# Sorting the last half lot of a mixture-of-experts layer through HBM instead of by matrix products

## The chip, the cores and the metric

The kernel runs on one core of one Trainium2 chip. The metric is the device time of one execution in microseconds (us), as the median over runs. TensorE (PE in the profile) multiplies matrices, VectorE (DVE) and ScalarE (ACT) do elementwise work, GpSimd (POOL) does a few elementwise operations and issues the indirect DMAs, and SyncE (SP) issues all plain DMAs of the main part. PEld is TensorE's weight load. A TensorE product of float32 leaves two records in the trace, a transpose one.

## The reference, cut to what matters

The input `x` is 8 sequences of 256 rows of 128 numbers, 2,048 rows in all. Four residual layers follow one another, each on a layer norm of its input: an attention with 8 heads (called a), a mixture of experts, a second attention with 16 heads (called b), and the same mixture of experts again with the same weights.

```python
x = x + attn_a(_layernorm(x, axis=-1), Mq, Mk, Mv)
x = x + ffn(_layernorm(x, axis=-1), w_gate, b_gate, W1, b1, W2, b2)
x = x + attn_b(_layernorm(x, axis=-1), wq, w_down, wk_up, wv_up, wo)
x = x + ffn(_layernorm(x, axis=-1), w_gate, b_gate, W1, b1, W2, b2)

def ffn(x, w_gate, b_gate, W1, b1, W2, b2):      # x_flat: rows of 128
    logits = x_flat @ w_gate + b_gate            # 8 experts
    probs = softmax(logits)
    route_p, route_idx = max(probs), argmax(probs)
    h = relu(einsum('nd,edm->enm', x_flat, W1) + b1[:, None, :])   # 512 wide
    y = einsum('enm,emd->end', h, W2) + b2[:, None, :]
    return y[route_idx, arange(n)] * route_p[:, None]
```

Only one expert's result is kept for a row, so the kernel computes each row for its own expert alone. For that the rows have to be put in order by expert, and the results have to be put back.

## The kernel before, in words

**Tiling.** The rows form four groups of 512 (two sequences, four tiles of 128 rows). Attention a runs over the groups, then attention b. A lot is what one call of `ffn_pieces` takes. The first mixture of experts takes each group as a lot (tiles named `..._f`). The second (`..._e`) takes groups 0, 1 and 2 as lots of four tiles, and group 3 as two half lots of two tiles, one for each sequence, as each sequence leaves attention b by itself. I call these five lots e0, e1, e2, e30 and e31. e31 is the last; `last` is true for it alone.

**A lot.** Layer norm (`layernorm_T`: `bn_stats`, a power on POOL that gives `rstd`, then `shift`, `hf` on ACT, transposes `pt`, a copy `hT`), gate products `pg`, a dozen small DVE operations that find each row's expert (`lg`, `mx`, `eq`, `sc`, `m2`, `sums`), two products `before` that count earlier rows of the same expert, and from them a place `ps_` for each row. Each expert has room for `CAP` rows (128 in a lot of four tiles, 64 in a half lot). A row that finds no room raises `over`, from which `find_most` (product `pov`) and `load_most` make a flag; if it is set, a branch at the end (`tc.If`) computes everything again without sorting. In the runs here that branch isn't taken.

**Sorting through HBM** (every lot but e31). `in_memory` makes two HBM buffers and writes zeros into the first (`tx`), by SP. POOL issues one indirect DMA for each tile that writes the rows of `h` to their places in `tx` (a put); SP loads `tx` back as `rows`, in order; `turned` transposes `rows` to `rTs` (products `prt`). Then come eight experts: `hidden` (products `H`, results `h1` on DVE or ACT) and `project` (products `py`, results `ys` on DVE). SP writes `ys` to the second HBM buffer (`ox`) in two halves, and POOL fetches each tile's results with an indirect DMA (`yg`, a gather). DVE adds them to the input (`x_e`), and SP stores the rows.

**Sorting by products** (e31 only, `sorted_here`). DVE compares a row of numbers (`place`) with each row's place and gives a matrix `has` of zeros and ones, 128 x 512 for each of the two tiles. Two products of `h` with `has` give the sorted, transposed rows at once. `has` is transposed (`pht`) and copied to `comes`; at the end, eight products `pn` of `comes` with `ys` put the results back. No HBM buffer, put, `rows` or gather is used. As `place` counts through experts with 64 places each, `ps_` is computed with `direct` (a step of 64 places between experts) instead of `region` (256).

**The order.** All instructions are issued in an order that is written out when the kernel is built. `Plan` holds an estimated clock for every engine and for DMA. Attention b is the main thread (`flow_b`); everything else, lots included, is a `Side`: a generator that yields the time at which its next piece is due. `fill` and `reach` step the ripe side of the best rank into the main thread. Where the plan's TensorE clock shows a gap, `busy` puts products of `ident` into a PSUM tile `spare`, whose result nobody reads. Each engine then runs its own list strictly in that order. So a change of a lot's steps changes the plan's clock, and with it the order and the spare products of everything after. `ranks[0] = rank` and `computed` hold a lot's experts back until the earlier lot's are done; `computed[0] < turn - 1` holds the load of `rows` back until the lot two before is done.

In attention b, `largest` and `exps` make score products (`S_b`, `ST_b`), DVE takes maxima (`top`), ACT exponentials (`bex`), `values` makes `acc_b`; `divide` turns `acc_b` into a new residual: ACT copies it to `both_b`, eight DMAs move the sums into `den_b` (in the last entry the products `pd_b` do this instead), DVE takes the reciprocal and forms `yT_b`, PE makes `py_b` and DVE `x_b`.

Of the kernel before, what the change touches and what calls it, by code (L numbers as in the profile page):

```python
# [24 lines left out]
def kernel(  # L25
# [29 lines left out]
    B, T, D = x.shape  # L55
    E, _, FF = W1.shape
# [149 lines left out]
    const = Pool("const", 1)  # L206
    xp = Pool("xp", 7)
    ln = Pool("ln", 2)
# [9 lines left out]
    class Ordered:  # L218
# [27 lines left out]
    PE, DVE, ACT, POOL = (  # L246
        Ordered(engine, name)
        for engine, name in (
            (nc.tensor, "pe"), (nc.vector, "dve"), (nc.scalar, "act"), (nc.gpsimd, "pool")
        )  # L250
    )

    def load(out, src):

        plan.dma(out, src, "sp")
        return tc.keep_in_program_order(nc.sync.dma_start(out, src))

    def misc(name):
        return pm.tile([P, 512], F32, tag="m", name=name)
# [60 lines left out]
    ident = const.tile([P, P], F32, tag="ident", name="ident")  # L320
# [3 lines left out]
    mark = const.tile([1, 1], F32, tag="mark", name="mark")  # L324
# [19 lines left out]
    ROWS = {4: 128, 2: 64}  # L344
# [2 lines left out]

    region = {n: const.tile([P, E], F32, tag=f"region{n}", name=f"region{n}") for n in ROWS}
    closer = {n: const.tile([P, E], F32, tag=f"closer{n}", name=f"closer{n}") for n in ROWS}
    direct = const.tile([P, E], F32, tag="direct", name="direct")  # L350
    place = const.tile([P, E * ROWS[2]], F32, tag="place", name="place")
    b1T = const.tile([P, E * NM], F32, tag="b1T", name="b1T")
    b2T = const.tile([P, E], F32, tag="b2T", name="b2T")
    nb1T = const.tile([P, E * NM], F32, tag="nb1T", name="nb1T")

    def setup_experts():
        steps = [(direct, ROWS[2])]
        for n, rows in ROWS.items():
            steps += [(region[n], n * P), (closer[n], rows - n * P)]
        for t, step in steps:  # L360
            DVE.tensor_scalar(t, first, -float(step), float(step * E), ALU.mult, ALU.add)
        count = mid.tile([P, E * ROWS[2]], I32, tag="both", name="count", bufs=1)
        POOL.iota(count, [[1, E * ROWS[2]]], base=0, channel_multiplier=0)
        POOL.tensor_copy(place, count)

        pb = misc("pb")
        PE.transpose(pb[:, 0 : E * NM], b_rows[: E * NM, 0, :], ident[: E * NM, : E * NM])
        PE.transpose(pb[:, 64 : 64 + E], b_rows[:E, 1, :], ident[:E, :E])
        ACT.copy(b1T, pb[:, 0 : E * NM])
        ACT.copy(b2T, pb[:, 64 : 64 + E])  # L370
        DVE.tensor_scalar(nb1T, b1T, -1.0, None, ALU.mult)
# [162 lines left out]
    def hop():  # L534

        return plan.end + plan.HOP
# [37 lines left out]
    def soon():  # L574
        return plan.at["pe"] + 1.0
# [328 lines left out]
    begun_ffn, computed, ended_ffn = [0], [0], [0]  # L904
# [24 lines left out]
    def in_memory(n, NL):  # L929
        to_expert = hbm.tile([E, NL * P, D], F32, tag=f"tx_{n}", name=f"tx_{n}")  # L930
        of_expert = hbm.tile([E * ROWS[NL], D], F32, tag=f"ox_{n}", name=f"ox_{n}")
        for nothing, to in by_expert(zeros.unsqueeze(1).to_broadcast([P, E, D]), to_expert):
            load(to, nothing)
        return to_expert, of_expert

    def ffn_pieces(turn, n, tokens, ended, vector_norm, ranks, rank, last):
        NL = sum(tiles for _, tiles in tokens)
        TL, CAP = NL * P, ROWS[NL]
        PT = 2 * CAP // P
        sorted_here = last  # L940
        if not sorted_here:
            to_expert, of_expert = in_memory(n, NL)
        while any(name not in x_of for name, _ in tokens) or turn - ended_ffn[0] >= LOTS:
            yield soon()
        h = ln.tile([P, ML, D], F32, tag="hf", name=f"hf_{n}", bufs=2)
# [5 lines left out]
        def row(name, dt=F32):  # L951
            t = sm.tile([P, ML], dt, tag=f"r{name}", name=f"{name}_{n}", bufs=LOTS)
            return t[:, 0:NL]
# [4 lines left out]
        def over_tiles(t, tiles=NL):  # L958
            return t.unsqueeze(1).to_broadcast([P, tiles, E])

        lg, d, sc, ex, rk = (small(s) for s in ("lg", "d", "sc", "gex", "rk"))
# [3 lines left out]
        eq = eqs[:, 0:NL, :]  # L965
# [17 lines left out]
        mx, m2, den, pr, ps_ = (row(s) for s in ("mx", "m2", "gden", "pr", "pos"))  # L983
# [14 lines left out]
        for lhsT, of, start in ((earlier, eqs, True), (ones, sums, False)):  # L998
            PE.matmul(
                before, lhsT=lhsT, rhs=of.rearrange("p n e -> p (n e)"), start=start,  # L1000
                stop=not start,
# [1 line left out]
        counts = before[:, NL * E : (NL + 1) * E]  # L1003
        DVE.tensor_tensor(
            rk, before[:, : NL * E].rearrange("p (n e) -> p n e", e=E),
            over_tiles(direct if sorted_here else region[NL]), ALU.add,
        )
        DVE.tensor_tensor(rk, rk, eq, ALU.mult)
        DVE.tensor_reduce(ps_, rk, AX.X, ALU.add)
        DVE.scalar_tensor_tensor(over, counts, -float(CAP), over, ALU.add, ALU.max)  # L1010
        if not sorted_here:
            pos = row("posi", I32)
            DVE.tensor_scalar(pos, ps_, float(E * TL - 1), None, ALU.min)
        if last:
            find_most()
        yield hop()
        if not sorted_here:
            puts = []
            for i in range(NL):

                POOL.memset(mark, 0.0)
                put = POOL.indirect_dma_start(
                    out=to_expert.rearrange("e c d -> (e c) d"),
                    out_offset=bass.IndirectOffsetOnAxis(ap=pos[:, i : i + 1], axis=0),
                    in_=h[:, i, :],
                    in_offset=None,
                )
                for other in puts:
                    tc.declare_no_dep(put.ins, other.ins, reason="rows of their own")
                puts.append(put)  # L1030
            yield hop()
            while computed[0] < turn - 1:
                yield soon()
            rows = ln.tile([P, E, D], F32, tag="rows", name=f"rows_{n}", bufs=3)
            for to, some in by_expert(rows, to_expert):
                load(to, some)
            loaded = hop()
            yield


        POOL.tensor_tensor(d, lg, wide(mx), ALU.subtract)
        if not sorted_here:
            POOL.tensor_tensor(rk, eq, over_tiles(closer[NL]), ALU.mult)
        yield hop()
        ACT.activation(ex, d, AF.Exp)
        if not sorted_here:
            DVE.tensor_reduce(m2, rk, AX.X, ALU.add)
            DVE.tensor_tensor(m2, m2, ps_, ALU.add)
            pos2 = row("posi2", I32)
            DVE.tensor_scalar(pos2, m2, float(E * CAP - 1), None, ALU.min)  # L1050
        yield hop()
        DVE.tensor_reduce(den, ex, AX.X, ALU.add)
        DVE.reciprocal(pr, den)
        yield None if sorted_here else loaded

        ranks[0] = rank
        while computed[0] < turn or not ready["bias"].over or not ready["turned"]:
            yield soon()
        rTs = {}
        if sorted_here:  # L1060

            has = ln.tile([P, NL, E * CAP], F32, tag="rows", name=f"has_{n}", bufs=3)
            for i in range(NL):
                DVE.tensor_scalar(has[:, i, :], place, ps_[:, i : i + 1], None, ALU.is_equal)
            yield hop()
            pt = misc(f"prt_{n}")
            for i in range(NL):
                PE.matmul(
                    pt, lhsT=h[:, i, :], rhs=has[:, i, :], start=(i == 0), stop=(i == NL - 1)
                )  # L1070
            rTs[0] = ln.tile([P, 512], F32, tag="rT", name=f"rT_{n}")
            ACT.copy(rTs[0], pt)
            yield
            comes = ln.tile([P, NL, E * CAP], F32, tag="rows", name=f"comes_{n}", bufs=3)
            for i in range(NL):
                pt = misc(f"pht_{n}_{i}")
                for k in range(E // 2):
                    PE.transpose(pt[:, ts(k, P)], has[:, i, ts(k, P)], ident)
                (DVE.tensor_copy, ACT.copy)[i % 2](comes[:, i, :], pt)
                yield  # L1080
        ys = ln.tile([P, E, D], F32, tag="rows", name=f"ys_{n}", bufs=3)
        stored = [0.0]

        def turned(t0):
            pt = misc(f"prt_{n}_{t0}")
            for i in range(4):
                PE.transpose(pt[:, ts(i, P)], rows[:, t0 + i, :], ident)
            copy = DVE.tensor_copy if vector_norm else ACT.copy
            rTs[t0 // 4] = ln.tile([P, 512], F32, tag="rT", name=f"rT_{n}_{t0}")
            copy(rTs[t0 // 4], pt)  # L1090

        def hidden(e):
            h1 = big.tile([P, NM, P], F32, tag="h1r", name=f"h1_{n}_{e}", bufs=4)
# [69 lines left out]
        if sorted_here:  # L1163
# [4 lines left out]
            for i in range(NL):  # L1168
                pn = misc(f"pn_{n}_{i}")[:, 0:D]
                for k in range(E // 2):  # L1170
                    PE.matmul(
                        pn, lhsT=comes[:, i, ts(k, P)], rhs=ys[:, k, :],
                        start=(k == 0), stop=(k == E // 2 - 1),
# [432 lines left out]
```

## Time and profile before

| what | value |
|---|---|
| time, median of 3 runs (lowest to highest) | 489.77 us (487.17 to 495.07) |
| time of the profiled execution | 486.11 us |
| its span, first to last instruction | 484.3 us |
| mean granted clock of TensorE | 0.994 |
| TensorE busy in slices 36 to 40 of 40 (tenths) | 8, 8, 8, 9, 6 |
| HBM traffic | 13.57 MB read, 10.88 MB written, 50 GB/s over the span |
| puts `tx_e`: issued on POOL, first to last start | 14, 305.8 to 439.1 us |
| gathers `yg_e`: on POOL, median us from issue to landing | 14, 2.5 us |
| layer norm's power on POOL for a half lot (`rstd_e`, 128x2) | 0.73 and 0.70 us |

A timeline line in the sections below gives start, duration, engine, line of the code, operation, output <- inputs, shapes and count; the bracket gives the engine's idle time before it and what ended that. All operations on PE, DVE, ACT and POOL bear line 227 (the helper `call` that records them) and all of SP's line 256, so groups are told apart by tile names. "SPq" is a DMA's issue on SP; the landing isn't in its duration.

### The profile page before, as it was taken

Reading aid. Unit: us, or ns where it says so; the run is one execution under the profiler, and the core shown is the slowest. Engines: PE = TensorE matmul, PEld = TensorE weight load, DVE = VectorE, ACT = ScalarE, POOL = GpSimd, SP = SyncE. Lnnn points to the kernel's source line nnn. Section 1 sums busy time; section 2 is a strip of 40 time slices with the busy share of each in tenths; the row PEclk is TensorE's granted clock in tenths of the full one; section 3 lists DMA queues with packets and bytes.
Section 4 is the critical chain, followed back from the end, with each engine's and each line's share of the span. In section 5 each row is a group of like instructions: output and inputs, shape, how many; then the busy total and the mean of one; then the engine's idle time right before and its main releaser. Section 6 shows DMA issues by size and latency. Waiting matters only on the chain.

```text
span 484.3 us, 13563 instructions
## 1 busy us (share of the span) xinstructions
PE 448.7 (93%) x5578; PEld 357.8 (74%) x5578; DVE 300.2 (62%) x816; ACT 223.2 (46%) x638; POOL 167.4 (35%) x249
## 2 busy tenths in 40 slices
PE   8899999999989899999999989989988999888996
PEld 7567775798567689787788667658776878577985
DVE  3555966953484937767756868667855867264231
ACT  2377454633364490456545446355634453242321
POOL 3032435542550565245430463413453002502310
PEclk9999999999999999999999999899999999999998
DMA  7980000103110002211131001010014101202210
GB/s 213 337 211 11 3 3 24 47 1 93 34 51 1 2 24 68 86 36 35 33 90 33 23 23 56 25 54 3 11 45 113 32 22 46 76 24 77 56 33 19
DMA packets 40550, 26.33 MB, mean 54 GB/s; under 512 B 3640, under 2 KB 37856, under 8 KB 40480
## 3 DMA queue, kind: packets, MB, share of 16 engines
q1 hardware_dynamic: 38560, 21.44, 15.2%
q0 software_dynamic: 1920, 3.94, 2.9%
q8 instruction: 46, 0.75, 0.6%
q14 instruction: 24, 0.20, 0.1%
HBM read 13.57 MB, written 10.88 MB: 50 GB/s over the span
## 4 chain that ended last, share of the span: by engine, by line
PE 68%; DVE 18%; ACT 8%; issue 4%; SPq 1%; POOL 0%; DMA 0%; another core or an unknown queue 0%; DVEq 0%; ACTq 0%; POOLq 0%
PE ST_b L227 8%; PE py_e L227 7%; PE H_e L227 6%; PE pq_a L227 6%; PE acc_b L227 5%; PE H_f L227 5%; PE S_a L227 4%; PE py_f L227 4%; PE spare L227 4%; PE S_b L227 3%; DVE nmax_a L227 3%; PE prot_b L227 3%; ACT ex_a L227 3%; DVE den_b L227 2%; DVE top L227 2%
## 5 line engine op out<-in xcount | busy, mean ns | idle before, releaser
L227 ACT ACTIVATE bex_b<-ST_b 128x768 f32<-128x768 f32 x64 | 51.9, 814 | 91.2 <-PE S_b L227 72.0
L227 DVE TENSOR_REDUCE top<-S_b 128x2 f32<-128x512 f32 (+1 forms) x128 | 65.1, 552 | 39.5 <-PE S_b L227 26.9
L227 ACT ACTIVATE ex_a<-S_a,nmax_a 128x256 f32<-128x256 f32 x128 | 58.9, 481 | 45.4 <-DVE nmax_a L227 37.7
L227 PE MATMUL ST_b<-qT_b,kT_b 32*128 32x128 f32 (+1 forms) x512 | 67.0, 352 | 4.2 <-issue 2.5
L227 PEld LDWEIGHTS ST_b<-qT_b,kT_b 32*128 32x128 f32 x512 | 49.5, 186 | 18.8 <-issue 9.7
L227 PE MATMUL S_b<-kT_b,qT_b 32*128 32x128 f32 (+1 forms) x512 | 59.8, 351 | 1.6 <-DVE top L227 1.5
L227 POOL TENSOR_TENSOR vh_a<-vs_a,rden_a 128x512 f32<-128x512 f32 x32 | 33.2, 1039 | 79.4 <-DVE rden_a L227 53.6
L227 PE MATMUL spare<-ident 128*128 128x128 f32 x364 | 51.2, 291 | 1.6 <-POOL ident masks.py:199 1.4
L227 PEld LDWEIGHTS spare<-ident 128*128 128x128 f32 x364 | 46.2, 202 | 5.0 <-issue 2.7
L227 PEld LDWEIGHTS S_b<-kT_b,qT_b 32*128 32x128 f32 x512 | 46.4, 186 | 4.5 <-issue 4.1
L227 DVE TENSOR_REDUCE nmax_a<-S_a 128x4 f32<-128x1024 f32 x32 | 38.7, 1211 | 13.3 <-PE S_a L227 13.2
L227 PE MATMUL H_e<-rT_e,W_sb 128*128 128x128 f32 (+1 forms) x320 | 40.7, 278 | 1.6 <-ACT rT_e L227 1.3
L227 PEld LDWEIGHTS H_e<-rT_e,W_sb 128*128 128x128 f32 x320 | 37.6, 192 | 3.8 <-ACT rT_e L227 1.8
L227 PE MATMUL S_a<-qT_a,kT_a 64*128 64x256 f32 x256 | 36.5, 402 | 2.5 <-ACT ex_a L227 1.6
L227 PE MATMUL py_e<-W_sb,h_e 128*128 128x128 f32 (+1 forms) x320 | 35.3, 278 | 0.9 <-DVE qT_b L227 0.9
L227 ACT ACTIVATE h_e<-H_e,b1T 128x128 f32<-128x128 f32 (+1 forms) x80 | 20.9, 350 | 32.3 <-PE H_e L227 32.3
L227 PE MATMUL H_f<-rT_f,W_sb 128*128 128x128 f32 x256 | 33.2, 280 | 2.0 <-DVE rt_b L227 1.1
L227 PEld LDWEIGHTS py_e<-W_sb,h_e 128*128 128x128 f32 (+1 forms) x320 | 32.4, 170 | 2.1 <-DVE qT_b L227 1.0
L227 PEld LDWEIGHTS H_f<-rT_f,W_sb 128*128 128x128 f32 x256 | 30.3, 192 | 4.6 <-issue 1.6
L227 PE MATMUL py_f<-W_sb,h_f 128*128 128x128 f32 x256 | 31.7, 278 | 0.4 <-issue 0.4
L227 PE MATMUL acc_b<-bex_b,vz 128*32 128x128 f32 (+1 forms) x512 | 29.9, 338 | 1.5 <-issue 1.4
L227 PEld LDWEIGHTS py_f<-W_sb,h_f 128*128 128x128 f32 x256 | 29.8, 192 | 1.6 <-issue 1.2
(220 smaller groups left out, 776.4 us busy)
## 6 DMA issues: line engine op xcount, KB each, us to landing
W_sb<-in_L_ffn_W_dram SPq DMA_DIRECT2D x16, 256.0 KB, 5.9
tx_f<-zeros SPq DMA_DIRECT2D x4, 512.0 KB, 6.9
rows_f<-tx_f SPq DMA_DIRECT2D x4, 512.0 KB
ox_f<-ys_f SPq DMA_DIRECT2D x8, 256.0 KB, 2.4
tx_e<-zeros SPq DMA_DIRECT2D x3, 512.0 KB
rows_e<-tx_e SPq DMA_DIRECT2D x3, 512.0 KB
ox_e<-ys_e SPq DMA_DIRECT2D x6, 256.0 KB, 2.5
x_in<-in_L_attn_a_x_dram SPq DMA_DIRECT2D x4, 256.0 KB, 3.7
```

Source lines behind the costliest of these rows:

```text
L227: return tc.keep_in_program_order(getattr(self.engine, op)(*args, **kw))
```

## The change

The last half lot gets its rows in order through HBM as the others do: `in_memory` is called for it, it makes puts, loads `rows` and transposes them with `turned(0)`. Its results still go by products: `has`, `comes` and `pn` stay. `has` now compares `place` with `m2` (the place in steps of 64, the sum of `ps_` and `closer`) instead of `ps_`; `direct` goes. `pos2`, the store to `ox` and the gathers stay left out for it. `turned` only moves upwards in the function.

```diff
-    direct = const.tile([P, E], F32, tag="direct", name="direct")
...
-        steps = [(direct, ROWS[2])]
+        steps = []
...
         sorted_here = last
-        if not sorted_here:
-            to_expert, of_expert = in_memory(n, NL)
+        to_expert, of_expert = in_memory(n, NL)
...
-            over_tiles(direct if sorted_here else region[NL]), ALU.add,
+            over_tiles(region[NL]), ALU.add,
...
-        if not sorted_here:
-            pos = row("posi", I32)
-            DVE.tensor_scalar(pos, ps_, float(E * TL - 1), None, ALU.min)
+        pos = row("posi", I32)
+        DVE.tensor_scalar(pos, ps_, float(E * TL - 1), None, ALU.min)
         if last:
             find_most()
         yield hop()
-        if not sorted_here:
-            puts = []
...
+        puts = []
+        for i in range(NL):
+
+            POOL.memset(mark, 0.0)
+            put = POOL.indirect_dma_start(
+                out=to_expert.rearrange("e c d -> (e c) d"),
+                out_offset=bass.IndirectOffsetOnAxis(ap=pos[:, i : i + 1], axis=0),
+                in_=h[:, i, :],
+                in_offset=None,
+            )
...
+        yield hop()
+        while computed[0] < turn - 1:
+            yield soon()
+        rows = ln.tile([P, E, D], F32, tag="rows", name=f"rows_{n}", bufs=3)
+        for to, some in by_expert(rows, to_expert):
+            load(to, some)
+        loaded = hop()
+        yield
...
-        if not sorted_here:
-            POOL.tensor_tensor(rk, eq, over_tiles(closer[NL]), ALU.mult)
+        POOL.tensor_tensor(rk, eq, over_tiles(closer[NL]), ALU.mult)
         yield hop()
         ACT.activation(ex, d, AF.Exp)
+        DVE.tensor_reduce(m2, rk, AX.X, ALU.add)
+        DVE.tensor_tensor(m2, m2, ps_, ALU.add)
         if not sorted_here:
-            DVE.tensor_reduce(m2, rk, AX.X, ALU.add)
-            DVE.tensor_tensor(m2, m2, ps_, ALU.add)
             pos2 = row("posi2", I32)
...
-        yield None if sorted_here else loaded
+        yield loaded
...
         if sorted_here:
+            turned(0)
+            yield
 
             has = ln.tile([P, NL, E * CAP], F32, tag="rows", name=f"has_{n}", bufs=3)
             for i in range(NL):
-                DVE.tensor_scalar(has[:, i, :], place, ps_[:, i : i + 1], None, ALU.is_equal)
+                DVE.tensor_scalar(has[:, i, :], place, m2[:, i : i + 1], None, ALU.is_equal)
             yield hop()
-            pt = misc(f"prt_{n}")
-            for i in range(NL):
-                PE.matmul(
-                    pt, lhsT=h[:, i, :], rhs=has[:, i, :], start=(i == 0), stop=(i == NL - 1)
-                )
-            rTs[0] = ln.tile([P, 512], F32, tag="rT", name=f"rT_{n}")
-            ACT.copy(rTs[0], pt)
-            yield
             comes = ln.tile([P, NL, E * CAP], F32, tag="rows", name=f"comes_{n}", bufs=3)
```

More of the change, by code (lines that the diff above doesn't have):

```diff
@@ L1016, in ffn_pieces @@
         yield hop()
-        if not sorted_here:
-            puts = []
-            for i in range(NL):
[L1021 to L1026, printed above, removed]
-                )
[L1028 to L1037, printed above, removed]
-            yield
+        puts = []
[7 more added lines that the diff above has]
+            )
+            for other in puts:
+                tc.declare_no_dep(put.ins, other.ins, reason="rows of their own")
+            puts.append(put)
+        yield hop()
[6 more added lines that the diff above has]
+        yield
         POOL.tensor_tensor(d, lg, wide(mx), ALU.subtract)
-        if not sorted_here:
-            POOL.tensor_tensor(rk, eq, over_tiles(closer[NL]), ALU.mult)
+        POOL.tensor_tensor(rk, eq, over_tiles(closer[NL]), ALU.mult)
         yield hop()
         ACT.activation(ex, d, AF.Exp)
+        DVE.tensor_reduce(m2, rk, AX.X, ALU.add)
+        DVE.tensor_tensor(m2, m2, ps_, ALU.add)
         if not sorted_here:
-            DVE.tensor_reduce(m2, rk, AX.X, ALU.add)
-            DVE.tensor_tensor(m2, m2, ps_, ALU.add)
             pos2 = row("posi2", I32)
@@ L1059, in ffn_pieces, with turned @@
         rTs = {}
+        def turned(t0):
+            pt = misc(f"prt_{n}_{t0}")
+            for i in range(4):
+                PE.transpose(pt[:, ts(i, P)], rows[:, t0 + i, :], ident)
+            copy = DVE.tensor_copy if vector_norm else ACT.copy
+            rTs[t0 // 4] = ln.tile([P, 512], F32, tag="rT", name=f"rT_{n}_{t0}")
+            copy(rTs[t0 // 4], pt)
         if sorted_here:
+            turned(0)
+            yield
             has = ln.tile([P, NL, E * CAP], F32, tag="rows", name=f"has_{n}", bufs=3)
             for i in range(NL):
-                DVE.tensor_scalar(has[:, i, :], place, ps_[:, i : i + 1], None, ALU.is_equal)
+                DVE.tensor_scalar(has[:, i, :], place, m2[:, i : i + 1], None, ALU.is_equal)
             yield hop()
-            pt = misc(f"prt_{n}")
-            for i in range(NL):
-                PE.matmul(
-                    pt, lhsT=h[:, i, :], rhs=has[:, i, :], start=(i == 0), stop=(i == NL - 1)
-                )
-            rTs[0] = ln.tile([P, 512], F32, tag="rT", name=f"rT_{n}")
-            ACT.copy(rTs[0], pt)
-            yield
             comes = ln.tile([P, NL, E * CAP], F32, tag="rows", name=f"comes_{n}", bufs=3)
@@ L1082, in ffn_pieces @@
         stored = [0.0]
[L1084 to L1090, printed above, removed]
         def hidden(e):
```

## The prediction

> **What bounds the kernel now.** I read the page's chain of waits first, then stage sums for the end of the run, then the timeline by engine from 383 us on. The chain:
>
> ```profile
> PE 68%; DVE 18%; ACT 8%; issue 4%; SPq 1%; POOL 0%; DMA 0%; another core or an unknown queue 0%; DVEq 0%; ACTq 0%; POOLq 0%
> ```
>
> TensorE's order sets the time; DMA and POOL carry nothing of it. The stages of the end (start:end, length, then busy us of PE, PEld, DVE, ACT, POOL with counts, granted clock, DMA share, GB/s):
>
> ```profile
> 422.35:446.27 23.92, 20.84 (x175) 19.65 (x174) 14.98 (x61) 8.01 (x26) 3.41 (x8) 1.00 0.14 40
> 446.27:460.74 14.47, 13.79 (x133) 12.84 (x133) 3.52 (x11) 4.22 (x17) 3.88 (x4) 1.00 0.23 65
> 460.74:464.64 3.90, 3.90 (x24) 2.85 (x24) 1.48 (x4) 0.59 (x1) 0.94 (x1) 1.00 0.11 34
> 464.64:480.00 15.36, 14.95 (x145) 14.04 (x143) 4.47 (x13) 4.23 (x17) 0.95 (x1) 1.00 0.08 21
> ```
>
> Attention b ends with `pd_b` at 422.3. Then come e2's experts, with the half lots' norm and gate beside them on other engines (23.92), e30's experts (14.47), e31's sorting by products (3.90), e31's experts and results (15.36), and 4.30 to the end of the span (484.3). PE is busy through all of it. What makes this possible is that e2's rows are in place by 422: POOL puts them (`tx_e`) before it fetches e1's results (`yg_e`), and both before the half lots' `rstd_e`:
>
> ```profile
> 407.97 1.05 POOL L227 DMA_INDIRECT tx_e<-hf_e,posi_e  x1 [16.46 <-issue]
> ...
> 411.86 0.96 POOL L227 DMA_INDIRECT tx_e<-hf_e,posi_e  x1 [0.22 <-issue]
> ...
> 413.54 1.02 POOL L227 DMA_INDIRECT yg_e<-ox_e,posi_e  x1 [0.16 <-issue]
> ...
> 417.37 0.94 POOL L227 DMA_INDIRECT yg_e<-ox_e,posi_e  x1 [0.30 <-issue]
> 421.14 0.73 POOL L227 TENSOR_TENSOR rstd_e<-ve_e,neg_half 128x2 f32<-128x2 f32 x1 [2.83 <-DVE m_e L227]
> ```
>
> One indirect DMA holds POOL for 1.26 (start to start), four for 4.8. SP's issues for e1's last results and e2's rows:
>
> ```profile
> 408.65 0.37 SPq L256 DMA_DIRECT2D ox_e<-ys_e  x1
> 414.16 0.37 SPq L256 DMA_DIRECT2D rows_e<-tx_e  x1
> ```
>
> One stretch is disturbed. ACT and DVE stand still until about the end of e1's last gather (418.3), by a releaser that the profile can't name:
>
> ```profile
> 418.09 1.51 ACT L227 ACTIVATE bex_b<-ST_b 128x768 f32<-128x768 f32 x2 [7.22 <-remote]
> ...
> 419.50 0.42 DVE L227 TENSOR_TENSOR x_b<-x_f,py_b 128x256 f32<-128x256 f32 x1 [7.59 <-remote]
> ```
>
> The last score product ends at 412.99, so this exponential could start at 413.05. With pieces at their usual length `pd_b` would have ended at 417.5 (exponentials to 414.6, two `acc_b` of 0.79 behind the spares to 415.9, three spares 0.66, `pd_b` 0.96): about 4.8 are lost.
>
> **What the diff itself costs.** Built, the changed program removes two products of `hf` with `has` (1.72 on the path at 461.89, four records of 0.59, pipelined) and has four transposes for them, 0.64 by the same step of e30 at 446.27. It adds two zero-writes on SP at 365.4 (1.36 by the e30 pair at 364.01; the next DMA behind them, `den_b`, waits for ACT until 372.8, so nothing), two puts (2.5) and a `rk` (0.23) on POOL ahead of e2's gathers, which wait for e2's results anyway, three DVE operations of 0.17 beside products, and two loads of e31's rows on SP (1.31 by e30's pair) behind e2's last results. They land some 12 before `prt` of e31 needs them. Alone, then, a gain of about 1. The flag's load to SP's register now stands ahead of e30's rows; the flag is ready at 435.4, those rows are needed at 449.7: nothing. The lost `direct` is one 0.15 operation in attention a.
>
> **What moves.** The extra zeros shift the plan's clock, and from 385 on the built order is another one. Up to `pd_b` PE does the same pieces, with 6 spare products where there were 14: 8 x 0.22 = 1.8 less (ten records took 1.12). But e2's norm, gate and counts (`pt`, `pg`, `before`) come two to three score steps later, and e1's experts 6 and 7 stand before them. POOL's list is turned round: e1's four gathers, then e2's four puts, then both `rstd_e`, then `d` and `rk` of e2, then the half lots' puts. PE's list after `pd_b` is: two spares, `py_b`, 31 spares, `pt` and `pg` of both half lots, and only then `prt` of e2. So e2's experts no longer cover the half lots' norm; 31 dummy products do.
>
> I walk through the new order, from PE at 383.3 where both programs still agree:
> - PE, with `py` pairs 1.86 to 1.98, a score step 0.87, `ptop` 0.37, one expert's `H` 0.89, `acc` 0.79, `py_b` and `pg` 0.9: `pt` of e2 waits for `hf` to 401.4, `pg` ends at 405.6, e1's last `py` at 408.7, the last score step at 410.4, e2's `before` at 411.7 and `pd_b` at 415.0. That is 2.5 before the undisturbed 417.5, 7.3 before the measured 422.3.
> - e1's last `ys` stands on DVE behind the division of the entry before (two reciprocals 1.75, `both` 0.74, `yT` 0.42, `sums` 0.73, from 407.4 on): it ends at 411.4, SP issues `ox` at 411.5. From issue to first gather the trace has 3.17 (446.04 to 449.21) and 2.58 (461.10 to 463.68); I take 2.9: gathers 414.4 to 419.2, e2's puts 419.5 to 424.3, `rstd` of e30 to 425.1, of e31 to 425.85.
> - e31's residual is ready earlier than that: `pd_b` 415.0, reciprocal 1.76, `both` 0.75, `yT` 0.42, `py_b` 0.5, `x_b` 0.41, statistics 1.2: 420.1. It waits 5 for POOL.
> - After `rstd`: `shift`, two `hf` 0.94, `pt`, `hT` 0.37, `gex` 0.23, the same for e31, both `pg` 0.9: 429.2. e2's rows: last put starts 423.3, load issued 2.3 later (411.86 to 414.16), landed 3.8 after that (packets until 418): 429.4. Both come together. `prt` starts at 429.4; before, it started at 422.15.
> - e2's experts: `prt` 0.64, `rT` 0.58, `H` 0.89; the half lots' DVE chains (8 operations of 0.205 each, 428.85 to 432.15, five for e30's places 1.0, `h_e` 0.63, six for e31 1.15) end at 435.0, and `pov` waits for them on PE; then seven `H`, four `py` pairs and a `prt`: 6.2 + 7.4 + 0.6. End 449.7, against 445.56.
> - e30's experts 14.47: 464.2. e31: `prt` 0.64, a wait for `has` (`ys` 0.29, `has` 0.45 each), `pht` 0.87, six spares 1.34: 467.3, that is 3.1 instead of 3.90. The rest as before, 15.36 + 4.30: 487.0.
>
> So the span goes from 484.3 to 487.0: e2 starts 7.3 later, of which its now undivided products give 3 back, and sorting gives 0.8. The profiled execution took 486.11 for its span of 484.3 (1.8 around it), so 488.8; it lies 3.7 below the median 489.77. On that scale the forecast is 492.5, rounded to 493 for hops of 0.02 to 0.1 that I haven't counted.
>
> The trace of before doesn't show a gather beside `divide`'s DVE chain. Its cost has the ends 0 (the gathers of e2 at 449 to 454: no engine stops) and 4.8 (those of e1 above). I take 0, since the 5 that e31 waits for POOL hide a part of it; 4.8 goes into the range. The wait from `ox` to gather, 2.58 to 3.3, moves the sum by 0.4.
>
> [...]
>
> **The rivals.** (a) Slower, 501: the standstill during gathers comes back in both places where gathers now meet other work. If DVE stops until 419.7, the division ends at 422.7, `py_b` at 423.2, and the 31 spares, which stand in PE's order behind it, run until 430.2 instead of giving way at 426.2: +4.0. If ACT and DVE stop at e2's gathers (now near 453 to 458, with e31's loads beside them) another 4.8. 492.5 + 8.8 = 501.3. It decides as soon as `py_b` of e31 ends after 419.3. For it: 7.2 and 7.6 of standstill in this trace. Against: smaller ones at other gathers (2.4 on DVE near 251, 0.7 on ACT at 289). With one of the two it is 496.5. (b) Faster, 482: e2's rows are there when attention b ends, so its experts again cover the half lots' norm: `pd_b` 415.0, then 23.92 + 0.7 + 14.47 + 3.1 + 15.36 + 4.30 = 476.9, with 1.8 and 3.7 added 482.4. Against it: POOL's built order has 10 of indirect DMAs between e1's last results and the half lots' `rstd`, and e2's rows behind them. (c) Nothing to tell, 489: the 3.7 between the profiled execution and the median are longer standstills of the same kind at e1's gathers, which the changed order doesn't have, as its score steps end before 414.4; then 488.8 stands without the 3.7.
>
> **How the numbers follow.** Two per cent, 9.8, is about what a measurement of this kernel can tell from no change; its three runs span 7.9. Forecast 493: 0.38. (a) with both stops: 0.31, with one: 0.15. (b) 0.06. (c) 0.10. Slower by over 2% (above 499.6) takes (a) with both stops and a part of one stop and of the forecast's own spread: 0.40. Faster by over 2% (below 480) is (b) with a little luck: 0.05. The rest, 0.55, lies within. The forecast's own range is 489 to 496; the range goes from 486 to 504, to take in (c) and (a) and leave out (b).
>
> **What would show it.** Right: e1's gathers before e2's puts on POOL, near 414 to 424; `rstd_e` near 425; a long row of `spare` between `py_b` and `pt_e`; `prt_e` of e2 near 429, 14 after `pd_b`; 3.1 between the experts of e30 and e31; no long standstill in the last score steps. Wrong: e2's `prt` waiting well past the gate (DMA bounds it), `remote` waits on DVE near 415 to 420 (a), or PE without gap after `pd_b` (b).

## The result and the profile after

| | before | after |
|---|---|---|
| median of 4 runs (lowest to highest) | 488.81 us (487.17 to 495.07) | 494.42 us (493.48 to 495.32) |
| profiled execution | 486.11 us | 494.35 us |
| its span | 484.3 us | 492.6 us |

The changed kernel is slower by 1.3%: ratio 1.0126, 95% interval 1.0084 to 1.0168. The forecast of 493 us was 1.4 too low. That closeness is partly luck: the span missed its forecast of 487.0 by 5.6, and the 3.7 added for the way from the profile to the median were not there. Some executions take over 1.5% longer than the fastest of the same kernel, at a lower granted clock (504.69 us at 0.959 against 490.20 at 0.985 for the kernel before on one chip), and the ratios leave these out.

The page's chain of waits for the changed kernel still begins with TensorE:

```profile
PE 69%; DVE 18%; ACT 7%; issue 3%; SPq 1%; DMA 0%; POOL 0%; another core or an unknown queue 0%; DVEq 0%; ACTq 0%; POOLq 0%
```

The stages of its end, as sums (columns as in the prediction; the column behind POOL is the granted clock):

```profile
374.00:379.00 5.00, 5.00 (x48) 4.51 (x41) 2.79 (x5) 1.01 (x2) 0.00 (x0) 0.66 0.08 23
...
418.25:421.40 3.15, 0.47 (x5) 0.30 (x4) 2.88 (x4) 0.00 (x0) 2.40 (x3) 1.00 0.16 42
421.40:430.60 9.20, 9.20 (x68) 9.18 (x68) 3.47 (x15) 0.88 (x2) 7.16 (x16) 0.81 0.23 73
430.60:434.90 4.30, 3.15 (x18) 2.66 (x17) 2.07 (x13) 1.64 (x6) 0.00 (x0) 0.79 0.44 122
434.90:439.40 4.50, 4.44 (x21) 4.03 (x21) 3.06 (x18) 0.58 (x1) 1.70 (x3) 0.50 0.04 16
439.40:444.20 4.80, 4.80 (x27) 4.80 (x28) 1.11 (x3) 0.99 (x4) 3.25 (x9) 0.59 0.30 92
444.20:455.40 11.20, 11.20 (x102) 11.18 (x101) 3.29 (x10) 3.95 (x15) 0.00 (x0) 1.00 0.09 26
455.40:470.00 14.60, 13.93 (x136) 12.97 (x135) 4.73 (x18) 4.35 (x18) 3.86 (x4) 1.00 0.30 83
470.00:473.00 3.00, 2.94 (x28) 2.78 (x27) 1.47 (x3) 1.17 (x2) 0.38 (x1) 1.00 0.15 44
```

`pd_b` ends at 418.25. Then PE waits, runs dummy products to 430.6 and sorts out norm and gate; e2's `prt` starts only at 433.8. The granted clock, 1.00 in every stage shown of before, is at half from 422.8 to 426.2 and from 433.1 to 443.3, and earlier once near 375 (near 304 both kernels have a stretch of it: 0.83 from 299 to 309 before, 0.72 after). POOL's timeline shows the turned list:

```profile
417.72 1.01 POOL L227 DMA_INDIRECT yg_e<-ox_e,posi_e  x1 [19.44 <-DMA ox_e<-ys_e]
...
422.82 1.00 POOL L227 DMA_INDIRECT tx_e<-hf_e,posi_e  x1 [0.23 <-issue]
...
426.70 0.97 POOL L227 DMA_INDIRECT tx_e<-hf_e,posi_e  x1 [0.23 <-issue]
427.70 0.74 POOL L227 TENSOR_TENSOR rstd_e<-ve_e,neg_half 128x2 f32<-128x2 f32 x1
...
428.49 0.71 POOL L227 TENSOR_TENSOR rstd_e<-ve_e,neg_half 128x2 f32<-128x2 f32 x1
```

Four gathers, four puts and only then both `rstd_e`, without a gap from 417.7 on: ten microseconds, as the forecast had it. On PE that looks so:

```profile
421.36 0.68 PE L227 MATMUL py_b<-wo_sb,yT_b 128*128 128x128 f32 x4 [2.69 <-DVE yT_b L227]
421.88 8.72 PE L227 MATMUL spare<-ident 128*128 128x128 f32 x62
430.44 0.38 PE L227 MATMUL pt_e<-ident,hf_e 128*128 128x128 f32 x2
431.79 0.71 PE L227 MATMUL pt_e<-ident,hf_e 128*128 128x128 f32 x2 [0.97 <-ACT hf_e L227]
...
433.77 1.09 PE L227 MATMUL prt_e<-ident,rows_e 128*128 128x128 f32 x4
...
435.54 2.08 PE L227 MATMUL H_e<-rT_e,W_sb 128*128 128x128 f32 x8
...
439.55 4.64 PE L227 MATMUL H_e<-rT_e,W_sb 128*128 128x128 f32 x24
```

The 31 dummy products (62 records) take 8.7 instead of 6.8 (31 at the prediction's 0.22), as part of them runs at half clock, 0.50 from 423 to 426; in after_again (below), at full clock, they take 7.09. No row of ACT or DVE between 395 and 480 has the long wait for `remote` that before has at 418 and 419.5.

### The profile page after: what moved, and what is told of

Read it like the earlier page. It is cut to its first block, busy times and chain, and to the rows that moved or that the text cites. A ratio compares the mean times of both kernels' runs of the same rounds, so it can differ in the third digit from the quotient of the medians.

```text
span 492.6 us, 13664 instructions
## 1 busy us (share of the span) xinstructions
PE 458.9 (93%) x5622; PEld 370.8 (75%) x5622; DVE 301.6 (61%) x818; ACT 223.6 (45%) x638; POOL 169.6 (34%) x254
## 4 chain that ended last, share of the span: by engine, by line
PE 69%; DVE 18%; ACT 7%; issue 3%; SPq 1%; DMA 0%; POOL 0%; another core or an unknown queue 0%; DVEq 0%; ACTq 0%; POOLq 0%
PE ST_b L227 8%; PE H_e L227 7%; PE py_e L227 6%; PE pq_a L227 6%; PE spare L227 5%; PE H_f L227 4%; PE acc_b L227 4%; PE S_a L227 4%; PE py_f L227 4%; PE S_b L227 3%; DVE nmax_a L227 3%; PE prot_b L227 3%; ACT ex_a L227 3%; DVE den_b L227 2%; DVE top L227 2%
## 5 line engine op out<-in xcount | busy, mean ns | idle before, releaser
L227 PE MATMUL ST_b<-qT_b,kT_b 32*128 32x128 f32 (+1 forms) x512 | 68.1, 356 | 4.9 <-ACT bex_b L227 2.9
L227 PE MATMUL spare<-ident 128*128 128x128 f32 x408 | 57.9, 297 | 1.4 <-POOL ident masks.py:199 1.4
L227 PEld LDWEIGHTS spare<-ident 128*128 128x128 f32 x408 | 53.5, 209 | 4.4 <-issue 2.2
L227 PE MATMUL H_e<-rT_e,W_sb 128*128 128x128 f32 (+1 forms) x320 | 44.2, 295 | 1.4 <-ACT rT_e L227 1.3
L227 PEld LDWEIGHTS H_e<-rT_e,W_sb 128*128 128x128 f32 x320 | 41.4, 209 | 3.4 <-ACT rT_e L227 1.8
L227 POOL DMA_INDIRECT yg_e<-ox_e,posi_e x14 | 13.5, 964 | 51.5 <-DMA ox_e<-ys_e 39.5
```

The costliest lines, as they stand in the source:

```text
L227: return tc.keep_in_program_order(getattr(self.engine, op)(*args, **kw))
```

## The experiments

The kernels were measured in four groups, each on one chip and each beside the kernel before. The chips turned out to matter: the kernel before takes 489 to 493 on some and 471 on others. So only ratios are compared. The first row is the result above, the last column tells the kind of chip; before_again is a single execution of the kernel before on the chip of after_again, for its trace, and has no ratio.

| run | ratio to before | 95% interval | before on that chip, us |
|---|---|---|---|
| changed kernel | 1.0126 | 1.0084 to 1.0168 | 488.8 |
| unbooked_zeros | 0.9982 | 0.9950 to 1.0013 | 491.9 |
| order_alone | 1.0103 | 1.0076 to 1.0131 | 491.9 |
| dummies_in_gaps | 1.0064 | 1.0034 to 1.0095 | 491.9 |
| late_gathers | 0.9984 | 0.9941 to 1.0028 | 491.9 |
| late_gathers_dummies | 0.9995 | 0.9956 to 1.0034 | 493.1 |
| after_again | 1.0211 | 1.0149 to 1.0273 | 471.2 |
| unbooked_again | 0.9915 | 0.9872 to 0.9957 | 471.2 |
| between_again | 0.9903 | 0.9863 to 0.9943 | 471.2 |
| gathers_between_rstd | 0.9917 | 0.9887 to 0.9947 | 470.7 |
| gathers_behind_e2 | 1.0118 | 1.0088 to 1.0148 | 470.7 |
| gathers_last | 0.9928 | 0.9906 to 0.9951 | 470.7 |

**The order or the step?** The first kernel makes the whole change, but hides two DMAs from the planner:

```diff
-            load(to, nothing)
+            if booked:
+                load(to, nothing)
+            else:
+                tc.keep_in_program_order(nc.sync.dma_start(to, nothing))
...
-        to_expert, of_expert = in_memory(n, NL)
+        to_expert, of_expert = in_memory(n, NL, not last)
```

> The changed kernel, but the two zero-writes of the last half lot are issued without being entered in the planner's account, so that all engines keep the order of the kernel before up to the experts of e30, and only the last half lot goes through HBM. Theory (the new order costs the time, the step through HBM itself saves about 0.8): ratio to before 0.998, from 0.994 to 1.003, that is 486 to 490 us beside a before of 488.8; 3.1 us between the experts of e30 and e31 instead of 3.90; e2's prt right behind pd_b; and the standstill of ACT and DVE during e1's gathers in the last score steps comes back, since the gathers stand there again. Rival (the two loads and two puts of the last half lot, and its rows in HBM, cost the time, not the order): ratio 1.008 or more, and e31's prt waiting for its rows.

The second does the reverse: before's work, with the planner charged.

```diff
+            if issued:
+                load(to, nothing)
+            else:
+                plan.dma(to, nothing, "sp")
...
         if not sorted_here:
             to_expert, of_expert = in_memory(n, NL)
+        else:
+            in_memory(n, NL, False)
```

> The kernel before, but the planner is charged with two zero-writes that are not issued. Nothing of the last half lot changes: it still goes by products. All engines take the order of the changed kernel from 385 us on. Theory (the order alone costs): ratio to before 1.014, from 1.009 to 1.019, about 495.5 us, that is the changed kernel plus the 0.8 to 1 that its last half lot saves; 31 dummy products ahead of pt, e1's gathers ahead of e2's puts. Rival (the step through HBM costs): ratio 0.997 to 1.004. Side question: the granted clock of the changed kernel was halved near 375 us after a PE wait of 1.86 beside four zero-writes; if those writes caused it, it is absent here and the time is up to 1.6 lower.

0.9982 and 1.0103: the step through HBM costs nothing that shows, and the order alone, with the last half lot still sorted by products, costs 1.0%. The theory holds, at the low end of its range for the second. The turned order is there in its trace, on PE and on POOL:

```profile
421.31 8.72 PE L227 MATMUL spare<-ident 128*128 128x128 f32 x62
```
```profile
421.32 0.96 POOL L227 DMA_INDIRECT yg_e<-ox_e,posi_e  x1 [0.30 <-issue]
...
422.58 1.00 POOL L227 DMA_INDIRECT tx_e<-hf_e,posi_e  x1 [0.22 <-issue]
```

The side question: its clock near 375 was not halved (16 records of `H` from 375.72 on take 1.95; in the changed kernel 3.31, from 374.71 on). In the order of before the standstill is back, on ACT and DVE of the kernel with unbooked zeros:

```profile
423.36 1.51 ACT L227 ACTIVATE bex_b<-ST_b 128x768 f32<-128x768 f32 x2 [8.79 <-remote]
...
423.40 0.42 DVE L227 TENSOR_TENSOR x_b<-x_f,py_b 128x256 f32<-128x256 f32 x1 [7.79 <-remote]
```

One number of the expectation was wrong: from the end of e30's products to e31's first `H` it takes not 3.1 but less than 2 (in unbooked_again 441.86 to 443.62, against 3.74 in before_again), since this build has one dummy product there, not seven (before has five). The step thus saves 2.0 here, a part of it by four dummy products fewer.

**The half clock.** Twelve more dummies are issued by `busy` ahead of the last `py_b`, seven ahead of e31's transposes; no other instruction is moved:

```diff
+    def issue_dummies(to):
+        for _ in range(dummies[0]):
+            tc.keep_in_program_order(
+                nc.tensor.matmul(to[:, 3 * P :], lhsT=ident, rhs=ident, start=True, stop=True)
+            )
+        dummies[0] = 0
...
             PE.matmul(spare[:, 0:P], lhsT=ident, rhs=ident, start=True, stop=True)
+        issue_dummies(spare)
...
+            if (g, b) == (groups[-1], 1) and len(groups) > 1:
+                dummies[0] = 12
...
+        if name == "e31_0":
+            dummies[0] = 7
+            issue_dummies(pt)
```

> The changed kernel with 12 more dummy products between pd_b and the last py_b and 7 between the transposes of e30 and of e31; every other instruction stands where it stood. In the changed kernel PE is idle there for 2.69 and 1.7 us, and the granted clock is 0.50 from 423 to 426 and from 433 to 443. Theory (the half clock, not the order alone, makes 3 to 4 of the 5.6 by which the span missed the forecast): no half clock between 419 and 445, the row of 31 dummies ends before hf of e30, so pt starts 0.7 earlier, H of e2's first expert takes 0.89 instead of 2.07 and the next 24 records 2.7 instead of 4.44; the time falls by 2 to 3.6, to a ratio of 1.006 (1.003 to 1.010) to before, about 491.5 us. Rival (those products wait for the DVE chains of the half lots anyway, by way of pov, so a faster clock only makes the wait longer): within 1 us of the changed kernel, ratio 1.011 to 1.015.

The ratio is the one expected, but the changed kernel's own ratio is from another chip, and its interval overlaps this one's. The trace supports the clock half of the story. PE's rows:

```profile
429.60 0.51 PE L227 MATMUL spare<-ident 128*128 128x128 f32 x3 [1.01 <-issue]
431.05 2.50 PE L227 MATMUL spare<-ident 128*128 128x128 f32 x14 [0.94 <-issue]
...
437.33 0.63 PE L227 MATMUL prt_e<-ident,rows_e 128*128 128x128 f32 x4
...
438.77 1.14 PE L227 MATMUL H_e<-rT_e,W_sb 128*128 128x128 f32 x8
...
442.24 2.84 PE L227 MATMUL H_e<-rT_e,W_sb 128*128 128x128 f32 x24
```

The first `H` takes 1.14 instead of 2.08, the next 24 records 2.84 instead of 4.64, and e2's experts 19.8 from `prt` to e30's `prt` (437.33 to 457.12) instead of 21.5 (433.77 to 455.22). But `pt` did not start earlier in this execution: the row of dummies itself stopped twice, for 1.01 and 0.94, at the end of e2's four puts (424.6 to 429.5) and with no releaser named, and one stretch at half clock came from about 431.8 to 435.2 (14 records of dummies take 2.50 from 431.05 on, another 14 take 2.42 from 433.76 on). So the clock's part in e2's experts, 1.7, is shown; the part in front of them isn't.

**The gathers.** Five kernels move e1's gathers on POOL. All hold them back with two lines at the head of the gather loop; late_gathers and late_gathers_dummies with these:

```diff
+            while n == "e1" and computed[0] <= turn + 1:
+                yield soon()
             yg = ln.tile([P, NT, D], F32, tag="yg", name=f"yg_{n}_{at}", bufs=1)
```

The others have `ended_ffn[0] <= turn` in that condition (behind those of e2, and last) or `("e", (NG - 1, 1)) not in x_of` (between the two `rstd`). late_gathers, gathers_between_rstd and gathers_last are built on the kernel with unbooked zeros, gathers_behind_e2 and late_gathers_dummies on the changed kernel.

> As the kernel with the unbooked zero-writes, but the gathers of e1's results wait until e2's experts have been issued, so that POOL runs e2's puts, both rstd of the half lots and their puts first, and no gather falls into the last score steps. Theory (ACT and DVE stand still because POOL gathers): no standstill of more than 2 us on ACT or DVE between 412 and 422, pd_b ends 4 to 5 earlier, and with e2's rows in place by 418 all later steps move with it: ratio to before 0.988, from 0.984 to 0.993, about 483 us. Rival (the standstill has another cause, or the saved time is given back since e2's rows or the half lots' norm come last): ratio 0.995 to 1.003, as the kernel with the unbooked zero-writes.

Here the rival won, and the trace says why. From e2's puts to the end of `pd_b` it took 10.3 (414.78 to 425.10) instead of 15.9 in the kernel with unbooked zeros: the standstill left that place. It went with the gathers. POOL, ACT, DVE and PE of this kernel:

```profile
444.10 0.98 POOL L227 DMA_INDIRECT yg_e<-ox_e,posi_e  x1 [0.30 <-issue]
...
447.92 0.94 POOL L227 DMA_INDIRECT yg_e<-ox_e,posi_e  x1 [0.30 <-issue]
...
450.43 0.58 ACT L227 COPY rT_e<-prt_e 128x512 f32<-128x512 f32 x1 [6.01 <-remote]
...
450.37 0.42 DVE L227 TENSOR_TENSOR ys_e<-py_e,bias 128x256 f32<-128x256 f32 x1 [2.64 <-remote]
...
446.45 0.60 PE L227 MATMUL prt_e<-ident,rows_e 128*128 128x128 f32 x4
451.07 7.09 PE L227 MATMUL H_e<-rT_e,W_sb 128*128 128x64 f32 x32 [4.01 <-ACT rT_e L227]
```

`prt` of e30 is done at 447.05, but ACT takes its copy up only at 450.43, 1.6 after the last gather. PE idles for 4.0, and the clock then stays at half for 10.2 (0.50 from 451 to 461): 32 records of `H` take 7.09 instead of 3.79.

> As the kernel with the unbooked zero-writes, but e1's gathers wait until the half lots' rows of attention b are complete, so that they stand on POOL between the rstd of e30 and that of e31, some 3 us behind e2's puts. In the run with late gathers the standstill went with the gathers to 447 to 450, where they followed the half lots' puts without a gap. Theory A (ACT and DVE stand still where four gathers follow puts directly): none of more than 2 us between 412 and 435, and nothing at 447: ratio to before 0.988, from 0.983 to 0.992, about 485 beside a before of 491. Theory B (gathers beside work that waits for PE bring the standstill anywhere): 3 to 5 us of standstill near 424 to 429, ratio 0.995 to 1.003.

> As the kernel with the unbooked zero-writes, but e1's gathers come behind e2's, eight in a row, some 5 us behind the last put. Theory A (standstill only where gathers follow puts directly): none, ratio to before 0.988, from 0.983 to 0.993, with up to 1.5 more for eight dummy products that the planner puts ahead of e31's experts. Theory B (gathers beside work that waits for PE): a standstill in e30's experts near 454 to 459, ratio 0.995 to 1.003. Theory C (more than some six indirect DMAs in a row): the same place and price as B here, but none in the kernel with the gathers between the two rstd.

Both were faster than before by 0.7 to 0.8%, but they ran on a chip where the kernel before takes 471 and where, as on another such chip (below), no trace has a wait for `remote`. They cannot tell theories A, B and C apart. Nor did the eight gathers of gathers_last stand in a row: four are at 434.5 to 439.2, four at 447.8 to 452.5.

> The changed kernel, but the gathers of e1's results wait on POOL until those of e2 have been issued, so that e2's puts stand first on POOL and both rstd of the half lots behind them. Up to pd_b every engine keeps the order of the changed kernel. Theory (in the new order it is POOL's turned list that costs: 10 us of indirect DMA between e1's last results and the half lots' rstd): e2's puts start near 416 instead of 422.8, rstd of e30 near 421 instead of 427.7, its rows are loaded near 423 instead of 429.9, e2's prt starts near 427 instead of 433.9, and the time falls by 5 to 7 below the changed kernel: ratio to before 1.000, from 0.995 to 1.004. Rival (the later norm and gate of e2, the division in front of the score steps and the two py pairs behind it cost, whatever POOL does): ratio 1.008 to 1.014.

By the ratio alone the rival won; against the changed kernel on another chip of this kind (1.0211, below) the theory is half right. `prt` follows `pd_b` by 8.7 (405.01 to 413.71), as expected, against 14.8 in after_again (404.71 to 419.48). Then two things ate 3.7 of the gain: half clock in e2's first experts (0.59 from 413 to 418, 0.50 from 418 to 423), which took 11.0 from the first `prt` to the second (413.71 to 424.75) instead of 9.2, and 28 dummy records of 3.29 ahead of e31's experts where after_again has 12 of 1.50.

> The kernel before, unchanged, for a second profile. In the last call its median was 470.7 us, in the call before that 491.9, and none of the three traces of the last call shows ACT or DVE standing still for more than 2 us without a releaser in the work itself, while all six earlier ones do, somewhere in attention b. Theory (the standstill comes with the device, not with the kernel's order alone): where this kernel takes about 490, its trace shows the standstill during e1's gathers again (4 to 6 us lost before pd_b); where it takes about 470, pd_b ends with no wait of more than 1 us in the last two score steps. Rival (the standstill depends on the order alone): it is there in both cases.

> The changed kernel, unchanged. Theory (the new order gives back the standstill of 4.8 that the kernel before has at e1's gathers, and costs some 10 besides): ratio 1.008 to 1.017 where the kernel before shows the standstill, 1.018 to 1.026 where it does not. Rival (the standstill plays no part in the ratio): 1.008 to 1.017 in either case. If the ratio is 1.018 or more in the place where the gathers moved behind e2's gave 1.0118, POOL's turned list is worth the difference; at 1.012 it is worth nothing.

> The changed kernel with the unbooked zero-writes, unchanged. Theory (same order as before, so the same standstill or none; the last half lot saves 0.8): ratio 0.995 to 1.002 in either case.

> The kernel with the gathers between the two rstd, unchanged. In the last call e2's experts took 21.4 in it, from prt to prt, where the first profile of before has 23.92, since the half lots' norm no longer waits for the gathers; with 0.7 for the last half lot that makes 3.2. Theory: ratio 0.990 to 0.995 where the kernel before shows no standstill, 0.980 to 0.988 where it does (the standstill of 4.8 goes as well). Rival (the standstill only moves, as in the run with late gathers): 0.990 to 1.000 there too.

PE in before_again, then in after_again, at the start of e2's experts:

```profile
404.45 1.13 PE L227 MATMUL pd_b<-both_b,swap 128*128 128x256 f32 x4
406.38 0.63 PE L227 MATMUL prt_e<-ident,rows_e 128*128 128x128 f32 x4 [0.80 <-DMA rows_e<-tx_e]
```
```profile
403.58 1.13 PE L227 MATMUL pd_b<-both_b,swap 128*128 128x256 f32 x4
...
408.36 7.09 PE L227 MATMUL spare<-ident 128*128 128x128 f32 x62
...
419.48 0.63 PE L227 MATMUL prt_e<-ident,rows_e 128*128 128x128 f32 x4 [0.22 <-DVE sc_e L227]
```

No trace on this chip has a wait for `remote`, in an order of PE that is that of the first trace of before: the order alone doesn't bring the standstill. That the chip brings it fits all groups; as each group ran once and on one chip, chip and occasion can't be told apart. Without the standstill the change costs 2.1%: 9.0 of span (468.1 to 477.1). The interval, 1.0149 to 1.0273, just meets that of the first measurement, 1.0084 to 1.0168. The unbooked kernel came out better than expected (0.9915 against 0.995 at best). 2.0 of its 4.0 are the shorter sorting of e31; for the rest these traces show only that the clock was halved twice, near 295 and 320, in before_again (mean 0.99) and not in unbooked_again (1.00). Moving the gathers between the `rstd` adds nothing on this chip (0.9903 against 0.9915).

The last kernel puts the findings together on the changed kernel: gathers late, and dummies in the waits.

> The changed kernel with e1's gathers behind the half lots' puts on POOL, 12 more dummy products between pd_b and the last py_b and 4 between the transposes of e30 and e31. With the gathers behind those of e2 the changed order started e2's experts 7 earlier after pd_b (8.7 instead of 14.8) but gave 1.9 back at half clock and 1.8 to sixteen more dummy records ahead of e31's experts. Theory (POOL's turned list is worth 7, once clock and dummies give nothing back): e2's prt 8 to 9.5 behind pd_b, no half clock in e2's experts, eight dummies ahead of e31's; ratio 1.003 to 1.009 where the kernel before takes about 470 and shows no standstill, 1.003 to 1.012 where it takes about 490 and the gathers may stop ACT and DVE after the puts. Rival (what costs lies before pd_b, in the division and the later norm): 1.011 to 1.016, with the 7 given back behind e2.

0.9995, a little better than the range. This chip is of the 490 kind. `prt` follows `pd_b` by 9.0, PE's rows run at full clock from 400 to 437 (16 records of `H` take 1.95 at 431.40 and at 435.58), and then, during the gathers (435.99 to 440.77), DVE and PE stand still once more:

```profile
440.16 0.42 DVE L227 TENSOR_TENSOR ys_e<-py_e,bias 128x256 f32<-128x256 f32 x1 [8.10 <-remote]
```
```profile
440.64 3.51 PE L227 MATMUL py_e<-W_sb,h_e 128*128 128x128 f32 x16 [3.11 <-issue]
```

The 1.3% of the change are gone without touching what it computes or its zero-writes. POOL's list and the clock, which this kernel alters together, were the price; how it divides between them on this kind of chip is not shown.

Only versions that keep the order of before up to the gathers are faster than before, and only on the 470 kind of chip is that shown: with unbooked zeros alone 0.9915 (0.9982, no difference, on the 490 kind); with the gathers between the two `rstd` as well, 0.9903 and 0.9917; with the gathers last 0.9928.

## Why the prediction was right, and where it was not

- **The diff is a small gain, the order is the cost.** Right, and shown by the first two runs. The gain of "about 1" is 2.0 where one dummy product stands in e31's sorting.
- **The term that was mis-sized most: PE's way to the end of `pd_b`.** Forecast 415.0, measured 418.25. I took 383.3 as a point up to which both programs agree; they agree in order, not in time. The first `py` pair that follows it starts at 385.1. At 355 both executions differ by only 0.2; the clock then fell to half from 375.0 to 378.5, behind a PE wait of 1.86 near 373 (0.66 in the row 374 to 379 above): sixteen records of `H` take 3.31 there instead of 1.95, which is most of the 1.8 lost between 355 and 385. The remaining 1.4 lie in the walk itself; 0.76 of it is `S_b` waiting for `top`, which stands on DVE behind the division of the entry before, a step that I had for `ys` and forgotten for `top`.
- **"zeros ... nothing".** Four zero-writes are in flight beside e0's gathers where there were two. In four of the five traces with four of them on the 490 kind of chip the clock is halved right behind, between 374 and 383 (sixteen records of `H` take 3.31 or 3.38, or four of `prt` 1.12), in neither of the two with two (1.95 for `H` at 374.36 and 375.72), and not in unbooked_again and between_again on the 470 kind (mean clock 1.00). That is a hint, not a proof.
- **From `pd_b` to `prt`.** Forecast 14.4, measured 15.5, and 14.77 on the chip without standstill. The mechanism, POOL's list turned round, is as forecast: ten of indirect DMA, `prt` gated by norm and rows together. Both gates came late: the dummies, a part of them at half clock, ended 0.8 behind `hf`, and SP issued the load of the rows at 429.90, 3.2 behind the start of the last put instead of 2.3; its last packet ends at 433.28. Dummies at full clock alone would thus have gained 0.5 at most.
- **The dummy products and the clock.** The sum took PE at full clock behind `pd_b`, with the 31 dummies in the gap. Wrong: half clock followed the 2.69 of waiting in front of them. Stretches at half clock are 3.4, 6.8 or 10.2 long in the traces of before, of the changed kernel and of late_gathers. Two of them followed waits of 1.86 and 2.69, but the same 2.69 in after_again (405.15 to 407.84) was not followed by one: the clock is 1.00 from 403 to 418 there, and the next stretch begins at 420.4. What decides is not shown.
- **e2's experts.** Forecast 20.3, measured 21.5, and 20.48 in after_again: the half clock again. "PE is busy through all of it" was too much for before: 20.84 of 23.92. Two sums of the working don't close: 435.0, 6.2, 7.4 and 0.6 make 449.2, not 449.7, and what the products "give back" is 3.8, not 3, if it is counted to e30's `prt` (446.27), as the span is.
- **The half lots.** e30 14.47 forecast, 14.4 measured; e30 to e31 3.1, measured 3.2; the rest 19.66, measured 19.9.
- **No standstill in the new order, neither at e1's gathers nor at e2's.** Right, so rival (a) fell. That the order of before has it, 4.8, held only on the 490 kind of chip. Without it the same change costs 2.1%: the forecast, 0.7% above before, owed its smallness to a stop that the kernel before doesn't always have.
- **3.7 from the profile to the median.** Wrong: with a fourth run before's median is 488.8, 2.7 above its profile, and after's profile equals its median. Rival (c) had that part right, the 3.7 being before's own (that longer standstills make it is not shown), but took the span of 487.0 for granted. Rival (b) fell with POOL's order.
- **The load of 512 KB, 3.8.** About right: in after_again `prt` starts 3.86 behind the load's issue (415.62 to 419.48), by the trace held last by DVE's `sc_e`; in the changed kernel the last packet ends 3.38 behind it (429.90 to 433.28). In before_again, where `prt` waits for this load, it is 4.44 (401.94 to 406.38).

## What to carry to other kernels

Where a planner writes the order of all engines, two more DMAs in its account, 0.7 us of SP's time each, cost 5 to 10 us here by moving a queue (1.0103 in order_alone, where they are never issued, to 1.0211 in after_again): book a new operation in a way that leaves the order alone, and compare the orders before the times. Look first at what a queue of indirect DMAs stands in front of; here 5 us of gathers that nobody awaited stood before puts and a power that everything awaited. And compare ratios from one chip only: the same change measured 1.3% on one and 2.1% on another.

## What the hardware showed unexpectedly

- **A standstill that comes with the chip or the occasion.** Where the kernel before takes 489 to 493, every trace has waits of ACT or DVE that end for `remote`, of 2.4 to 8.8 us in all traces but that of the changed kernel (0.7). Each of the long ones lies in a series of gathers and ends within 1.6 us of the last gather's end (251, 290, 372, 418, 423, 440, 450); in three traces (unbooked_zeros, order_alone, late_gathers) ACT has one of 1.9 that ends near 215, where the trace of before has a series of puts (209.7 to 214.5). On the chips with 471 no trace has one. Not every series does it: e2's four gathers never did. What decides it, and what signal comes late, stays open; puts directly in front are not needed, since e0's gathers in the kernel with unbooked zeros follow their puts by 5 us and stopped ACT for 4.2.
- **The two kinds of chip differ at series of puts or gathers without such a wait, too.** PE has one and the same order in both traces of the kernel before, so they can be laid side by side. PE falls behind by 16.3 us in all: 7.07 of it up to 208.90, 12.2 up to 374.09, mostly without a row that names `remote` (0.84 from 208.90 to 215.75, over the puts of 209.67 to 214.53), then 4.5 at e2's puts and e1's gathers (12.21 at 408.09, 16.75 at 420.43), and nothing at e2's gathers (16.29 at 446.27 and at 460.67). POOL's first gathers of e1 start at 413.54 and 401.33. In the two traces of the changed kernel it is 15.3 in all, but nothing at e1's gathers (13.52 at 417.10 and at 421.36), where PE waits and runs dummies.
- **The clock fell after short waits and stayed down for 10.2 us while PE was busy** (half clock from 433.1 to 443.3 in the changed kernel, behind 3 us with PE idle for 1.1 of them, and with PE busy for 9.24 of the 9.30 from 434.9 to 444.2).
